# A graph network on one core: landing times in the planner, filled waits in front of bank sums, and a mask by TensorE

## The chip, the cores and the metric

The kernel runs on one core of a Trainium2 chip. A core has engines that run side by side, each with its own queue in order: TensorE (PE; its weight loads are shown as PEld), VectorE (DVE), ScalarE (ACT), GpSimd (POOL) and SyncE (SP), which here issues every DMA. They meet through semaphores. TensorE writes to PSUM banks; the other operands lie in SBUF. The metric is the device time of one execution in microseconds, as the median of several runs. The profile is one further execution with every instruction recorded.

## The reference

128 graphs of 128 nodes with 256 features each pass through two layers, all in f32.

```python
h = relu(layernorm(x))                       # layer 0: three steps of a gated network
for i in range(3):
    m = h @ weight[i]
    aggr = A^T @ m                           # A = (adj != 0), 128 x 128 per graph
    gi, gh = aggr @ w_ih.T + b_ih, h @ w_hh.T + b_hh
    r, z = sigmoid(i_r + h_r), sigmoid(i_z + h_z)
    n = tanh(i_n + r * h_n)
    h = (1 - z) * n + z * h
x = x + h
h = relu(layernorm(x))                       # layer 1: attention
Wh = h @ W.T
s1, s2 = Wh @ a1, Wh @ a2
e = leaky_relu(s1[:, None] + s2[None, :], 0.2); e = where(adj == 0, -inf, e)
x = x + softmax(e) @ Wh
```

The adjacency is symmetric and has its diagonal set.

## The kernel before

The graphs are worked on in 32 groups of four (`G = 4`, `NG = 32`; 512 columns, two halves of `H = 256`). A group g has a prologue (first norm, adjacency turned into 0 and 1, state transposed to columns), three steps `gru_step` (layers l = 0, 1, 2), and an epilogue (second norm and attention).

**A step.** The gates come from products of stationary 128x128 blocks with 256 moving columns (L705). Each 2x2 block product is done with seven products instead of four (as in Strassen's scheme), with sums in PSUM banks: `blocks` fills the banks `u` and `m7`, ScalarE copies `m7` out (L728), VectorE adds `c2 = u + m` (L731) and later `c22 = u + m` (L740). The bank `u` is written again by the next product, so each sum must have read it before. VectorE then adds halves of the candidate (`add_half`, L800), ScalarE applies tanh (L758, L793, L658), and VectorE makes the new state in three passes (L663, L665, L667). The sums' operands (`moving_sums`, L470) are VectorE's too. Steps of different groups are interleaved by a fixed plan (a step of layer l of group g stands at `3 g + 4 l`).

**Trips by way of DRAM.** A full transpose is made of 32x32 transposes on VectorE and a trip to DRAM and back (`by_way_of_dram`): four DMAs write z, four read it back. So go the state (`z_a`, `z`, `z_b`; writes of 128 KB) and the exponentials of the attention (`squares_by_blocks`, L586: `z_e<-prT`, then `e<-z_e`; writes of 64 KB). The gather on TensorE that reads e is `pq` (L614), and the last products `po` (L1063) follow. Groups 29, 30 and 31 (`late`) transpose on TensorE instead, without a trip; 30 and 31 (`end`) use tiles of other work, and 31 (`final_one`) goes in two halves of two graphs.

**The planner.** The order of instructions on all engines is written out at build time by `Order`, a list scheduler in Python with its own account of durations. Each piece of work is a generator that yields (engine, length, earliest start, tile to be free) ahead of each instruction; `begin` says when it could start, `take` books it, `issue` lets the generator go on. `HOP` is 0.2, `LAND` 2.5 us. `gru_step` drives it: after each product it fills with other tasks (`fill`, `matmuls`), by start and rank (`better`); the bank sums are booked with `take`, in the place of the program that they have. The account decides the order alone. At run time an instruction waits for what it needs, and whatever stands behind it in its queue waits too. What matters below: after its four writes `by_way_of_dram` sets the reads' earliest start to the last write plus `LAND`, and returns the last read plus `LAND`, whatever the size; `squares_by_blocks` adds 2.0 to that.

**Attention's mask.** `epilogue` makes scores with VectorE (L946), spreads them over the rows, adds the two and applies the leaky relu on ScalarE (L983); L992 turns A into 0 or -1e30, L994 adds it to e, L1000 takes the rows' maximum, L1004 the exponentials. In the last group relu is taken of x minus its mean alone (`norm_scales(..., True)`: L429, with the power on POOL, L431, beside it), and the scale rstd comes in later: in L946 and in the copies L1022.

Of the kernel before, what the change touches and what calls it, by code (L numbers as in the profile page):

```python
# [10 lines left out]
AF = mybir.ActivationFunctionType  # L11
ALU = mybir.AluOpType
# [5 lines left out]
G = 4  # L18
# [9 lines left out]
def preln_gnn_kernel(  # L28
# [144 lines left out]
    class Order:  # L173
# [18 lines left out]
        def take(self, engine, length, ready, room=None, count=1):  # L192
# [8 lines left out]
            return done  # L201

        def open(self, room, name):
            self.room_of[name] = room, self.next[room]
            self.next[room] = (self.next[room] + 1) % len(self.rooms[room])
            if room == "misc" and self.room_of[name][1] > 2:

                return more[self.room_of[name][1] - 3].rearrange("p n t -> p (n t)")
            if room == "misc":
                return ps_misc.tile([P, T], F32, tag="misc", name=name)  # L210
            if room == "h":
                return work.tile([P, G, D], F32, tag="h", name=name, bufs=ROWS)
# [66 lines left out]
        def finish(self, tasks=None, enough=lambda: False):  # L279

            tasks = self.tasks if tasks is None else [t for t in tasks if t[2] is not None]
            while tasks and not enough():
                best = None
                for task in self.tasks:
# [3 lines left out]
                    if engine == PE and start > self.free[PE] + 0.1 and task not in tasks:  # L288
                        continue
                    if self.better((start, rank), best):  # L290
# [121 lines left out]

    def norm_scales(src, graphs, ready, name, apart=False):

# [11 lines left out]
        put(nc.vector.tensor_scalar_add(rstd[:, all_], mv[:, all_, 1], EPS))  # L426
        if apart:
            t2 = yield DVE, 0.08, t - HOP
            put(nc.vector.tensor_scalar(nb[:, all_], mv[:, all_, 0], -1.0, None, ALU.mult))  # L429
            t = yield POOL, 1.05, t  # L430
            put(nc.gpsimd.tensor_tensor(rstd[:, all_], rstd[:, all_], mhalf[:, all_], ALU.pow))  # L431
            return rstd, nb, t2, t
        t = yield POOL, 1.05, t
# [7 lines left out]
    def norm_apply(src, graphs, rstd, nb, ready, name, kept, room="h"):  # L441

        for k in graphs:
            t = yield (ACT, 0.5, ready) if kept else (ACT, 0.5, ready, room)
            if not kept:
# [5 lines left out]
            put(nc.scalar.activation(  # L451
                h[:, k, :], src[:, k, :], AF.Relu, bias=nb[:, k : k + 1],
                scale=rstd[:, k : k + 1] if rstd is not None else 1.0,
            ))
# [60 lines left out]
    def by_way_of_dram(tmp, to, n, ready, name, room=None):  # L515

        z = None
        for i in range(Q):
# [3 lines left out]
            dma(z[:, :, i, :], tmp[i * 32 : (i + 1) * 32])  # L522
        order.close(f"tq_{name}" if n > G else f"prT_{name[:-2]}", t + LAND)
        ready = t + LAND
        rows_ = z.rearrange("r (q n) i a -> q r (n i a)", q=Q)
        to_ = None
        for q in range(Q):
# [3 lines left out]
            dma(to_[q * 32 : (q + 1) * 32], rows_[q])  # L531
        return t + LAND

# [48 lines left out]
    def squares_by_blocks(e, prT, ready, name):  # L582
# [5 lines left out]
        ))  # L588
        t = yield from by_way_of_dram(
            tmp.rearrange("p q k a -> p (q k) a"), lambda: e.rearrange("p k s -> p (k s)"),  # L590
            G, t, f"{name}_e",
        )
        return t + 2.0

# [59 lines left out]
    def state(s, o, old, new, v, z, ready):  # L654
# [5 lines left out]
        if len(s.halves) == C:  # L660
# [10 lines left out]
            if s.l < NL:  # L671
# [3 lines left out]
                if s.due:  # L675
                    s.task = order.add(0, inputs(s, s.hT_ready))
            else:

                for graphs in [range(G)] if s.g < NG - 1 else [range(2), range(2, 4)]:
                    order.add((1.8 if s.g >= NG - 2 else 1.9 if s.g == NG - 3 else 2), epilogue(s, graphs, max(s.halves)))  # L680

    def gru_step(s, last):
# [34 lines left out]
        def blocks(no, gates):  # L717
# [11 lines left out]
            done = product(gates, lambda q: u[:, q, :], S2, None, T2, t, False, (DVE,))  # L729
            t = order.take(DVE, 0.62, max(done, tm, banks["c2"]))  # L730
            put(nc.vector.tensor_tensor(c2, u, m, ALU.add))  # L731
# [6 lines left out]
            order.fill(t, (DVE,))  # L738
            tc22 = banks["u"] = order.take(DVE, 0.62, t)
            put(nc.vector.tensor_tensor(c22, u, m, ALU.add))  # L740
# [57 lines left out]
        def add_half(o, cols, src, ready):  # L798
            t = order.take(DVE, 0.38, max(ready, s.v_ready))
            put(nc.vector.tensor_tensor(v[:, o, cols], v[:, o, cols], src, ALU.add))  # L800
            return t
# [18 lines left out]
    class Group:  # L820


        def __init__(self, g):
            self.g, self.l, self.entered, self.aT = g, 0, False, None
            (self.xt, _), (self.at, self.at_ready) = xts.pop(g), ats.pop(g)
            self.scales = scales.pop(g)
            self.kept, self.prT = [], None
            self.e = self.hs = None
            self.due = False
# [29 lines left out]
    def prologue(s):  # L859
# [18 lines left out]
        if s.entered:  # L878
            s.task = order.add(0, inputs(s, s.hT_ready))

    def place_of_e(g):
        if g < NG - 2:
# [5 lines left out]
    def epilogue(s, graphs, ready):  # L888
# [21 lines left out]
        for i, two in enumerate(twos(graphs)):  # L910
# [7 lines left out]
            else:  # L918
                put(nc.vector.tensor_add(x1[:, k2, :], x1[:, k2, :], h[:, k2, :]))
        if final_one:  # L920

            rstd, nb, t, t2 = yield from norm_scales(x1, graphs, t - HOP, f"b{name}", True)
        else:
            rstd, nb, t = yield from norm_scales(x1, graphs, t - HOP, f"b{name}")
        h, t = yield from norm_apply(
            x1, graphs, None if final_one else rstd, nb, t, f"b{name}", s.kept,
            "tq" if end else "h",
        )
        if final_one:
            t = max(t, t2)  # L930

# [4 lines left out]
        for i in (1, 0):  # L936
            for k in graphs:
# [4 lines left out]
                if s.prT is None:  # L942
# [3 lines left out]
                put(nc.vector.scalar_tensor_tensor(  # L946
                    unused, h[:, k, :], rstd[:, k : k + 1] if final_one else 1.0, wa[:, i, :],
                    ALU.mult, ALU.mult,
                    accum_out=(one, two)[i][:, k : k + 1],
                ))  # L950

        if late:
            t = yield PE, graph_t, t, "misc"
            p2 = order.open("misc", f"ps2_{name}")
            for k in graphs:
                put(nc.tensor.transpose(
                    p2[:, k * P : (k + 1) * P], two[:, k : k + 1].to_broadcast([P, P]), ident
                ))
# [29 lines left out]
        le = e[:, part, :]  # L988

        off_ready = yield DVE, 0.36 * n / G, ready  # L990
        off = s.A[:, part, :]
        put(nc.vector.tensor_scalar(off, off, -1.0, BIG, ALU.add, ALU.mult))  # L992
        t = yield DVE2, row_t, max(t, off_ready) - HOP
        put(nc.vector.tensor_tensor(le, le, off, ALU.add))  # L994
        if s in live:
# [228 lines left out]
```

## Time and profile before

| | |
|---|---|
| Time, median of 3 runs | 2139.99 us (2139.34 to 2142.39) |
| The profiled execution: its own time | 2139.41 us |
| its span, first to last instruction | 2137.6 us |
| TensorE busy | 2117.2 us, 99% |
| VectorE busy | 1726.6 us, 81% |
| ScalarE busy | 1301.4 us, 61% |
| GpSimd busy | 103.5 us, 5% |
| DMA packets, bytes | 667973, 211.92 MB |
| mean granted clock of TensorE | 0.997 |

In the lines that follow, a row names an engine, a line of the kernel, the operation, the tile written and the tiles read, and their shapes; then how often, busy time and mean duration. A waiting row names who waited for whom, the total, how many times and the longest. In the order of time each row begins with its start and its length; brackets hold the engine's idle time before it and what ended it. SPq is SP's queue: the length there is the issue, not the transfer. Two matmul records belong to one f32 product, one to a transpose.

### The profile page before, as it was taken

The numbers are of one execution on the slowest core, as the hardware profiler recorded it, in microseconds if no ns is written. First come the engines' busy times: TensorE is split into PE (matmuls) and PEld (weight loads), VectorE is DVE, ScalarE is ACT, GpSimd is POOL, SyncE is SP. The second block draws the span as 40 slices with busy tenths as digits, with TensorE's granted clock in tenths as the row PEclk, the third lists the DMA queues.
The fourth block names the chain that finished last, engine by engine and source line by source line (L and its number), as shares of the span: only waits on it lengthen the run. The fifth ranks groups of instructions, "written<-read, shape, count | busy, mean of one in ns | idle before, by whom it ended". The sixth has DMA issues, their size and how long they took to land. (4 is left out here: it accounts for less than half of the span.)

```text
span 2137.6 us, 32105 instructions
## 1 busy us (share of the span) xinstructions
PE 2117.2 (99%) x10763; PEld 1878.8 (88%) x10763; DVE 1726.6 (81%) x3767; ACT 1301.4 (61%) x2855; POOL 103.5 (5%) x200
## 2 busy tenths in 40 slices
PE   9999999999999999999999999999999999999997
PEld 7888888888888888888888888888888888888886
DVE  7777888888878788878888787888778887787777
ACT  6556566565656566656656565666566565665664
POOL 1000000000000000000000000000000000000000
PEclk9999999999999999999999999999999999999998
DMA  5333453636353544545263536445462635344301
GB/s 158 64 85 83 88 117 70 154 65 141 90 121 73 133 96 94 125 111 119 56 149 82 120 72 137 88 98 122 95 133 64 146 82 107 84 88 108 84 19 46
DMA packets 667973, 211.92 MB, mean 99 GB/s; under 512 B 578336, under 2 KB 644640, under 8 KB 667808
## 3 DMA queue, kind: packets, MB, share of 16 engines
q1 hardware_dynamic: 667808, 209.87, 44.0%
q8 instruction: 85, 1.39, 0.3%
q14 instruction: 80, 0.66, 0.1%
HBM read 121.91 MB, written 87.88 MB: 98 GB/s over the span
## 5 line engine op out<-in xcount | busy, mean ns | idle before, releaser
L793 ACT ACTIVATE z<-c,brz 128x256 f32<-128x256 f32 x384 | 185.0, 482 | 305.4 <-PE c L705 158.5
L705 PE MATMUL u<-t_h,s_hh 128*128 128x256 f32 x1152 | 343.4, 380 | 0.3 <-DVE c L731 0.3
L705 PE MATMUL u<-t_a,s_f 128*128 128x256 f32 x1152 | 311.3, 379 | 0.0
L705 PE MATMUL c<-aT,s_f 128*128 128x256 f32 x1152 | 311.3, 379 | 0.0
L758 ACT ACTIVATE r<-c,brz 128x256 f32<-128x256 f32 x384 | 175.2, 477 | 207.7 <-PE c L705 127.3
L731 DVE TENSOR_TENSOR c<-u,m 128x512 f32<-128x512 f32 x192 | 134.0, 698 | 142.0 <-PE u L705 132.6
L705 PEld LDWEIGHTS u<-t_a,s_f 128*128 128x128 f32 x1152 | 218.9, 190 | 29.7
L705 PEld LDWEIGHTS c<-aT,s_f 128*128 128x128 f32 x1152 | 218.9, 190 | 29.7
L705 PEld LDWEIGHTS u<-t_h,s_hh 128*128 128x128 f32 x1152 | 216.7, 190 | 31.3 <-DVE c L731 2.2
L800 DVE TENSOR_TENSOR v<-v,c 128x256 f32<-128x256 f32 x384 | 154.4, 420 | 109.5 <-ACT z L793 55.3
L705 PE MATMUL c<-hT,s_hh 128*128 128x256 f32 x768 | 228.4, 379 | 0.0
L736 ACT COPY c<-u 128x512 f32<-128x512 f32 x192 | 109.4, 570 | 123.5 <-PE u L705 122.2
L728 ACT COPY m<-m 128x512 f32<-128x512 f32 x192 | 112.4, 585 | 105.1 <-PE m L705 105.1
L765 ACT ACTIVATE v<-c,bhn 128x256 f32<-128x256 f32 x384 | 172.1, 476 | 0.0
L705 PE MATMUL m<-t_h,s_hh 128*128 128x256 f32 x576 | 171.5, 379 | 0.0
L705 PE MATMUL c<-t_h,s_hh 128*128 128x256 f32 x576 | 171.3, 379 | 0.0
L740 DVE TENSOR_TENSOR c<-u,m 128x512 f32<-128x512 f32 x192 | 132.2, 688 | 42.3 <-ACT c L736 40.6
L705 PEld LDWEIGHTS c<-hT,s_hh 128*128 128x128 f32 x768 | 145.2, 190 | 19.4
L705 PE MATMUL m<-t_a,s_f 128*128 128x256 f32 x576 | 155.7, 379 | 0.0
L705 PE MATMUL u<-aT,s_f 128*128 128x256 f32 x576 | 155.7, 379 | 0.0
L705 PE MATMUL c<-t_a,s_f 128*128 128x256 f32 x576 | 155.6, 379 | 0.0
L652 DVE SCALAR_TENSOR_TENSOR v<-r,v 128x1024 f32<-128x1024 f32 x96 | 117.4, 1223 | 21.6 <-ACT v L765 20.0
(161 smaller groups left out, 3894.4 us busy)
## 6 DMA issues: line engine op xcount, KB each, us to landing
z<-tq SPq DMA_DIRECT2D x248, 128.0 KB
h<-z SPq DMA_DIRECT2D x248, 128.0 KB
xt<-in_x SPq DMA_DIRECT2D x31, 512.0 KB
z_a<-tq_a SPq DMA_DIRECT2D x120, 128.0 KB
hT_a<-z_a SPq DMA_DIRECT2D x120, 128.0 KB
z_b<-tq_b SPq DMA_DIRECT2D x116, 128.0 KB
h_b<-z_b SPq DMA_DIRECT2D x116, 128.0 KB
x<-in_x SPq DMA_DIRECT2D x29, 512.0 KB
```

Of the source, the lines that this page charges most:

```text
L652: put(nc.vector.scalar_tensor_tensor(flat(v), flat(r), 1.0, flat(v), ALU.add, ALU.mult))
L705: put(nc.tensor.matmul(to(q), S[0][:, gate_no, weight, :], moving, start=first and q == 0 and i == 0, stop=(i == len(ends) - 1), skip_grou ...
L728: put(nc.scalar.copy(m, m7))
L731: put(nc.vector.tensor_tensor(c2, u, m, ALU.add))
L736: put(nc.scalar.copy(c1[1], u))
L740: put(nc.vector.tensor_tensor(c22, u, m, ALU.add))
L758: put(nc.scalar.activation(r[:, o, cols], src, AF.Tanh, bias=brz[:, o : o + 1], scale=0.5))
L765: put(nc.scalar.activation(v[:, o, cols], src, AF.Identity, bias=bhn[:, o : o + 1], scale=0.5))
L793: put(nc.scalar.activation(z[:, o, cols], src, AF.Tanh, bias=brz[:, C + o : C + o + 1], scale=0.5))
L800: put(nc.vector.tensor_tensor(v[:, o, cols], v[:, o, cols], src, ALU.add))
```

## The change

**Landing by size.** `by_way_of_dram` sets the reads' earliest start to 3.7 us after the last write for trips of state (128 KB) and 1.8 us for e (64 KB), and returns 2.7 us after the last read; `squares_by_blocks` adds nothing to it any more.

**Filled waits.** A new `Order.fixed` books an operation whose place is given, but first issues other tasks of the same engine that end by the time at which it could begin, plus 0.1 us. The sums L731 and L740 and `add_half` use it. In `finish` a TensorE task that isn't ready is put last instead of being passed over.

**Mask by TensorE for groups 30 and 31.** A task `mask` makes A into 0 or -1e30 for the whole group, planned for 5 us before the last state half. `epilogue` puts a product of the identity with that A into the bank of the scores, and the scores are added to it by products instead of transposes; ScalarE reads the sum. For the other groups the mask stands as it did; group 29's scores are products too. VectorE's addition L994 falls away for 30 and 31.

**The last group's norm** is that of the others again: relu has the scale and the offset, L946 and the copy of the exponentials have none, and the copy is one for two graphs.

```diff
@@ class Order
+        def fixed(self, engine, length, ready):
+            while True:
+                until = ready + HOP
+                best = None
+                for task in self.tasks:
+                    if task[2][0][:3] != engine[:3]:
+                        continue
+                    start = self.begin(task[2][0], *task[2][2:])
+                    if start + task[2][1] <= until + 0.1 and self.better((start, task[0]), best):
+                        best = start, task[0], task
+                if best is None:
+                    return self.take(engine, length, ready)
+                self.issue(best[2])
@@ finish
                     if engine == PE and start > self.free[PE] + 0.1 and task not in tasks:
-                        continue
+                        start += 1000.0
@@ norm_scales
-        if apart:
-            t2 = yield DVE, 0.08, t - HOP
-            put(nc.vector.tensor_scalar(nb[:, all_], mv[:, all_, 0], -1.0, None, ALU.mult))
-            t = yield POOL, 1.05, t
-            put(nc.gpsimd.tensor_tensor(rstd[:, all_], rstd[:, all_], mhalf[:, all_], ALU.pow))
-            return rstd, nb, t2, t
@@ by_way_of_dram
-        order.close(f"tq_{name}" if n > G else f"prT_{name[:-2]}", t + LAND)
-        ready = t + LAND
+        ready = t + (3.7 if n > G else 1.8)
+        order.close(f"tq_{name}" if n > G else f"prT_{name[:-2]}", ready)
...
-        return t + LAND
+        return t + 2.7
@@ squares_by_blocks
-        t = yield from by_way_of_dram(
+        return (yield from by_way_of_dram(
...
-        return t + 2.0
@@ state
+                if s.g >= NG - 2:
+                    s.off_ready = INF
+                    order.add(1, mask(s, max(s.halves) - 5.0))
@@ blocks (the same for c22), add_half
-            t = order.take(DVE, 0.62, max(done, tm, banks["c2"]))
+            t = order.fixed(DVE, 0.62, max(done, tm, banks["c2"]))
...
-            t = order.take(DVE, 0.38, max(ready, s.v_ready))
+            t = order.fixed(DVE, 0.38, max(ready, s.v_ready))
@@ new
+    def mask(s, ready):
+        t = s.off_ready = yield DVE, 0.36, ready
+        put(nc.vector.tensor_scalar(s.A, s.A, -1.0, BIG, ALU.add, ALU.mult))
+        return t
@@ epilogue
-        if final_one:
-            rstd, nb, t, t2 = yield from norm_scales(x1, graphs, t - HOP, f"b{name}", True)
-        else:
-            rstd, nb, t = yield from norm_scales(x1, graphs, t - HOP, f"b{name}")
+        rstd, nb, t = yield from norm_scales(x1, graphs, t - HOP, f"b{name}")
...
-                    unused, h[:, k, :], rstd[:, k : k + 1] if final_one else 1.0, wa[:, i, :],
-                    ALU.mult, ALU.mult,
+                    unused, h[:, k, :], 1.0, wa[:, i, :], ALU.mult, ALU.mult,
...
         if late:
-            t = yield PE, graph_t, t, "misc"
+            t = yield PE, 4 * graph_t if end else graph_t, max(t, s.off_ready), "misc"
             p2 = order.open("misc", f"ps2_{name}")
+            if end:
+                put(nc.tensor.matmul(
+                    p2[:, cols], ident, s.A[:, part, :].rearrange("p k s -> p (k s)"),
+                    start=True, stop=False, skip_group_check=True,
+                ))
             for k in graphs:
-                put(nc.tensor.transpose(
-                    p2[:, k * P : (k + 1) * P], two[:, k : k + 1].to_broadcast([P, P]), ident
+                put(nc.tensor.matmul(
+                    p2[:, k * P : (k + 1) * P], two[:, k : k + 1].to_broadcast([P, P]), ident,
+                    start=not end, stop=True, skip_group_check=True,
                 ))
...
-        off_ready = yield DVE, 0.36 * n / G, ready
-        off = s.A[:, part, :]
-        put(nc.vector.tensor_scalar(off, off, -1.0, BIG, ALU.add, ALU.mult))
-        t = yield DVE2, row_t, max(t, off_ready) - HOP
-        put(nc.vector.tensor_tensor(le, le, off, ALU.add))
+        if not end:
+            off_ready = yield from mask(s, ready)
+            t = yield DVE2, row_t, max(t, off_ready) - HOP
+            put(nc.vector.tensor_tensor(le, le, s.A, ALU.add))
...
+            t = yield ACT, bank_t, t
+            order.close(f"pp_{name}", t)
             prT = s.prT
-            if not final_one:
-                t = yield ACT, bank_t, t
-                put(nc.scalar.copy(prT[:, part, :].rearrange("p k s -> p (k s)"), pp[:, cols]))
-            else:
-                ready = t
-                for k in graphs:
-                    t = yield ACT, 0.3, ready
-                    put(nc.scalar.activation(
-                        prT[:, k, :], pp[:, k * P : (k + 1) * P], AF.Identity,
-                        scale=rstd[:, k : k + 1],
-                    ))
-            order.close(f"pp_{name}", t)
+            put(nc.scalar.copy(prT[:, part, :].rearrange("p k s -> p (k s)"), pp[:, cols]))
```

More of the change, by code (lines that the diff above doesn't have):

```diff
@@ L410, in preln_gnn_kernel, with norm_scales @@
     s_hh, s_f = (stationary_tile("hh"), {}), [(stationary_tile(f"f{l}"), {}) for l in range(NL)]
-    def norm_scales(src, graphs, ready, name, apart=False):
+    def norm_scales(src, graphs, ready, name):
         st = small.tile([P, G, 6], F32, tag="st", name=f"st_{name}", bufs=2)
@@ L451, in norm_apply @@
             put(nc.scalar.activation(
-                h[:, k, :], src[:, k, :], AF.Relu, bias=nb[:, k : k + 1],
-                scale=rstd[:, k : k + 1] if rstd is not None else 1.0,
+                h[:, k, :], src[:, k, :], AF.Relu, bias=nb[:, k : k + 1], scale=rstd[:, k : k + 1]
             ))
@@ L588, in squares_by_blocks @@
         ))
-        t = yield from by_way_of_dram(
+        return (yield from by_way_of_dram(
             tmp.rearrange("p q k a -> p (q k) a"), lambda: e.rearrange("p k s -> p (k s)"),
             G, t, f"{name}_e",
-        )
-        return t + 2.0
+        ))
     def rows(s, ready, name):
@@ L738, in blocks @@
             order.fill(t, (DVE,))
-            tc22 = banks["u"] = order.take(DVE, 0.62, t)
+            tc22 = banks["u"] = order.fixed(DVE, 0.62, t)
             put(nc.vector.tensor_tensor(c22, u, m, ALU.add))
@@ L826, in __init__ @@
             self.scales = scales.pop(g)
+            self.off_ready = 0.0
             self.kept, self.prT = [], None
@@ L919, in epilogue @@
                 put(nc.vector.tensor_add(x1[:, k2, :], x1[:, k2, :], h[:, k2, :]))
-        if final_one:
-            rstd, nb, t, t2 = yield from norm_scales(x1, graphs, t - HOP, f"b{name}", True)
-        else:
-            rstd, nb, t = yield from norm_scales(x1, graphs, t - HOP, f"b{name}")
+        rstd, nb, t = yield from norm_scales(x1, graphs, t - HOP, f"b{name}")
         h, t = yield from norm_apply(
-            x1, graphs, None if final_one else rstd, nb, t, f"b{name}", s.kept,
-            "tq" if end else "h",
-        )
-        if final_one:
-            t = max(t, t2)
+            x1, graphs, rstd, nb, t, f"b{name}", s.kept, "tq" if end else "h"
+        )
         v = small.tile([P, 2, G], F32, tag="s", name=f"s_{name}")
@@ L952, in epilogue @@
         if late:
-            t = yield PE, graph_t, t, "misc"
+            t = yield PE, 4 * graph_t if end else graph_t, max(t, s.off_ready), "misc"
             p2 = order.open("misc", f"ps2_{name}")
+            if end:
+                put(nc.tensor.matmul(
+                    p2[:, cols], ident, s.A[:, part, :].rearrange("p k s -> p (k s)"),
+                    start=True, stop=False, skip_group_check=True,
+                ))
             for k in graphs:
-                put(nc.tensor.transpose(
-                    p2[:, k * P : (k + 1) * P], two[:, k : k + 1].to_broadcast([P, P]), ident
+                put(nc.tensor.matmul(
+                    p2[:, k * P : (k + 1) * P], two[:, k : k + 1].to_broadcast([P, P]), ident,
+                    start=not end, stop=True, skip_group_check=True,
                 ))
```

## The prediction

> **What bounds the kernel now.** I read the page first, for the engine that is full; then TensorE's waits, for the places where it isn't; then the order of time around the largest kind of wait; then windows of the last 30 us.
>
> ```profile
> span 2137.6 us, 32105 instructions
> PE 2117.2 (99%) x10763; PEld 1878.8 (88%) x10763; DVE 1726.6 (81%) x3767; ACT 1301.4 (61%) x2855; POOL 103.5 (5%) x200
> ```
>
> TensorE is busy for 99% of the span. A busy PE need not be at its peak, so I checked the work behind it. Six passes of a 128x256 product stand in 1.29 us in the chain, 0.2157 us each; an f32 product has two passes, 0.431 us, a 128x128 one 0.222 us, a transpose one pass of 0.111 us. A group of four graphs has 3 x 42 products for the steps (18.1 us each step, 54.4), 24 for the sums over neighbours (5.3), 8 for the attention (1.8) and 8 for the output (3.5): 64.9 us, and 32 groups fill the span. So only TensorE's waits and what stands at both ends can be won. VectorE's idle time is mostly in front of the bank sums (132.6 us until L705), but L731 held TensorE up once, for 0.3 us.
>
> ```profile
> engine line waited for: us in total, times, longest us
> PE pq L614 <- DMA e<-z_e: 5.9, 6, 1.7
> PE c L956 <- DVE prT L946: 4.4, 1, 4.4
> PE u L504 <- DVE hT L667: 3.7, 1, 3.7
> PE pw L362 <- DMA wih<-in_w_ih_t: 1.4, 2, 1.2
> ```
>
> The first row is in the middle of the kernel, the next two are the end. The order of time around the longest of the six, and around a trip of another group that waits for nothing:
>
> ```profile
> 1288.07 0.70 DVE L586 STREAM_TRANSPOSE prT<-e 128x512 f32<-128x512 f32 x1
> 1288.51 2.50 SPq L60 DMA_DIRECT2D hT_a<-z_a  x4
> ...
> 1292.15 2.49 SPq L60 DMA_DIRECT2D h<-z  x4
> 1294.74 3.52 SPq L60 DMA_DIRECT2D z_e<-prT  x4
> ...
> 1300.07 1.70 SPq L60 DMA_DIRECT2D e<-z_e  x4
> ...
> 1303.93 0.35 PE L614 MATMUL pq<-e,h_b 128*128 128x128 f32 x1 [1.74 <-DMA e<-z_e]
> ...
> 1172.26 0.70 DVE L586 STREAM_TRANSPOSE prT<-e 128x512 f32<-128x512 f32 x1
> 1172.99 2.92 SPq L60 DMA_DIRECT2D z_e<-prT  x4
> 1176.64 2.87 SPq L60 DMA_DIRECT2D z<-tq  x4
> 1179.69 2.40 SPq L60 DMA_DIRECT2D e<-z_e  x4
> ```
>
> In the first, the transpose is done at 1288.8 but SP still has another group's writes and reads in hand, and the writes of e go out 6.7 us after the transpose's start instead of 0.7. The six trips that wait are those where SP was 6 to 7 us late (groups 7, 10, 13, 16, 19, 22). In the second, SP is free; e's last read is issued 9.8 us after the transpose, and TensorE takes e 14.4 us after it without a wait.
>
> ```profile
> 2105.00:2111.00 6.00, 2.40 (x12) 1.76 (x10) 5.63 (x13) 1.27 (x3) 0.00 (x0) 1.00 0.00 0
> 2111.00:2113.00 2.00, 1.56 (x12) 1.29 (x12) 1.95 (x6) 0.26 (x1) 0.00 (x0) 0.88 0.00 0
> 2113.00:2117.00 4.00, 0.00 (x0) 0.00 (x0) 3.81 (x12) 2.04 (x7) 0.89 (x1) 0.50 0.00 0
> 2119.00:2122.40 3.40, 3.40 (x10) 2.64 (x9) 2.52 (x11) 2.30 (x7) 0.84 (x1) 0.50 0.16 57
> ```
>
> These are windows (us, then PE, PEld, DVE, ACT, POOL, then the granted clock). The last product of the last step ends at 2105.5; VectorE is then full while TensorE idles twice, the granted clock falls to 0.50, and eight passes of po take 3.41 us in the chain instead of 1.73. From 2105.5 to the span's end are 32.1 us, for 16.6 us of TensorE's work.
>
> **The change, part by part.**
>
> *Accounts of writes.* Nothing in an instruction changes; the planner's order does, and each trip's 8 DMAs go with it. In the new order of instructions I counted TensorE's products between the one that VectorE's transpose stands behind and the first product that reads e. Before, it is 14.2 to 16 us by group, with z_e behind other groups' trips in every third. After, groups 1 to 26 all have 16.0 us and one SP order: z_e, z of another state (128 KB), e, h. That is the second excerpt, which nine trips already have, none with a wait. Its margin: reads issued by +10.0 us at worst, landing 1.7 to 2.8 us after the last issue (the six late trips), product at +14.4: 1.6 us to spare. The queue that z_e was moved past is SP's, which is free then: its preceding load comes some 20 us earlier. So the six waits go. Their worth: 5.9 us of rows, but from group 5's transpose to group 23's (584.00 to 1761.58) are 1177.6 us for 18 x 64.93 = 1168.7 us of products, a difference of 8.9, of which 1.2 may be the rounding of the pass (0.1%): 7.7 lost. Between 5.9 and 7.7 I take 7.2, as each wait seems to cost 0.2 more than its row. What is late next: the trips of h have 26 us or more of products in front of them (21 before). Group 27 is bunched: z_e between two writes of z_b, and only 12.2 us to its product against some 10 to 11 us of trip: 0 to 1.2 us, I take 0.4.
>
> *Filling in front of bank sums.* It moves work within VectorE; the same instructions remain. TensorE pays only if a sum comes late: it is read 0.32 us after the sum's end in nearly every case. The fill lets work end 0.1 us after the sum could begin; walking VectorE's order with the rows' durations, one sum per group (behind four L470 at 0.45 us) lands where eight of before landed, which TensorE awaited by 0.05 us at most. So 0 to 1.2 us in all, I take 0.1, and 0.2 for the first 60 us, where VectorE's order is a little longer.
>
> *Mask by TensorE.* Removed behind L946: L992, L994 (0.42 and 0.69 for four graphs, 0.28 and 0.43 for two), now one row of 0.42 per group, made earlier (for group 31 right behind hT, ahead of the maximum of 30's e). Added: the mask's products, 0.86, 0.43 and 0.43 us, and twelve transposes of scores turned into two-pass products, 12 x 0.11: 3.1 us of TensorE's work. No row of before has this mask product; the nearest is L705's width, 0.216 us a pass of 256, and twice that for 512. The product waits for A alone; behind it on TensorE stand the scores, then attention of group 29.
>
> *Scale taken back into the last group's norm.* The relu waits for POOL's three operations, some 0.7 to 0.9 + 0.27 + 0.2 us, instead of none: about 1.2 us later. The two scaled copies L1022 (0.63) become one of 0.37. Cover of the 1.2: TensorE's po of groups 29 and 30, 3.4 us, which the new order puts before the last scores. Without that cover, +1.2.
>
> *The end, summed.* Before the last product of a step, TensorE has 2088.4 us of products where it had 2089.7: 1.3 earlier. Then, from that product's end: mask and scores of 30, attention of 29 to 3.5 us; idle to 6.0 (v, z and two tanh to 2.4, then three passes of hT at 1.14 and the hop; before, 5.6); transposes and po of 29 to 8.6; e of 30 to 9.1; a copy, idle to 10.0; attention of 30, po of 29 and 30 to 15.2 without a gap; scores of 31 to 16.1, po of 30 to 17.8, scores of its second half and e to 18.9; then three short waits for copies (0.7 each) and 5.5 us of products to 26.4. With the 3.4 us that stand between TensorE's last product and the end of the span now, 29.8 us, against 32.1: 2.3 won.
>
> *The clock, row against rule.* In before the clock fell after 3.74 us idle plus 1.6 us of transposes. The Trainium skill (TensorE: Matmul & The Clock Gate, What's actually happening) says that half clock comes after at least one idle window of about 3.4 us, and (Part 4: PE-mode transpose) that transposes do not count as busy like products. After the change the stretch is 2.45 us idle and 0.9 us of transposes, 3.3. By the row (5.3 us fell) nothing is said of 3.3; by the rule it stands just under the bound, and the window runs free, so it mostly holds. Full clock gives the 29.8 above; half clock adds 1.7, the row's 3.41 less 1.73. I take full clock.
>
> Sum: 2137.6 - 7.2 - 1.3 - 2.3 + 0.4 + 0.1 + 0.2 = 2127.5 us of span. The profiled execution took 2139.4, 1.8 more than its span, and the median of the runs is 0.6 over it: 2129.9.
>
> **Rivals.**
>
> *The end gives nothing* (20%). The clock falls, or VectorE's longer queue (hT behind three scores and an output row) moves the idle times rather than shortening them: then 2.3 to 4 us come back, 2132 to 2134. For it: a stretch of 3.3 us so near the window; VectorE 5.63 of 6 us busy. Against: more of TensorE's work stands ready for the hole, 3.5 us for 1.7.
>
> *Waits of e return in part* (7%): SP's trips land more slowly where they now follow each other, half of the 7.2 stays and group 27 costs 1.2: 2134 to 2137. Against: the nine trips.
>
> *A wait in each group, slower* (5%). The account for e's writes allows 1.8 + 2.7 us where it allowed 7. If e now lands later than 14.4 us after its transpose in every period, 27 trips make TensorE wait. Each wait costs its length and 0.2; it decides at 10.1 / 27 = 0.37 us a group, a landing at 14.6 us; with waits of 0.7 us it is 2129.9 + 27 x 0.9 = 2154. Against: 1.6 us to spare in the nine.
>
> *It does nothing* (3%): the planner's order is fixed by TensorE, fills are off its path: 2139 to 2141. The fills alone are this; the change of SP's order is not.
>
> **How the numbers follow.** The likeliest, all of the sum, has 65%, with 2126 to 2132 of its own (at the one end 7.7 won by the waits and 5.0 at the end, if half of the 5.4 us of idle time that my walk leaves there goes too; at the other 5.9 and 1.5, with all extras). About 0.2%, 4.3 us, is what a measurement can tell from no change: faster means under 2135.7. That holds for the likeliest, the first rival and half of the second: 0.89. Within: the rest of the second and the third's nothing, 0.06. Slower 0.05. The range, 2125.5 to 2135, has 0.5 below that for the median's own spread and leaves out the last two rivals and half of the second.
>
> **What would show it.** TensorE's row for e<-z_e at 0 to 1 us, and only group 27 in it. Every z_e issued 0.7 us after its transpose. The row c L731 under 1.5 us. At the end one idle stretch near 2.5 us in place of 3.7 and 4.4, granted clock 1.00 in it, and the span's end 29 to 31 us after the last product of a step. The forecast is wrong if the row of e grows to a wait per group, if bank sums hold TensorE for several us, or if the clock halves.

## The result, and the profile after

The changed kernel takes 2128.83 us (median of six, 2128.43 to 2129.86) beside 2140.05 us (2138.60 to 2144.93) for the kernel before: 0.9944 of it, with an interval of 0.9931 to 0.9957. The forecast was 2129.9. The total was right. The reason given for its largest part was not, and one term at the end was a matter of chance.

The head of the page of the changed kernel; its profiled execution took 2129.86 us, 1.8 more than its span:

```profile
span 2128.1 us, 32183 instructions
PE 2117.1 (99%) x10781; PEld 1885.4 (89%) x10781; DVE 1723.9 (81%) x3761; ACT 1300.5 (61%) x2853; POOL 101.9 (5%) x204
```

TensorE's waits after the change (who waited for whom, us in total, times, longest):

```profile
PE u L513 <- DVE hT L676: 2.5, 1, 2.5
PE pw L378 <- DMA wih<-in_w_ih_t: 1.5, 2, 1.3
PE c L623 <- ACT prT L1033: 1.2, 2, 0.7
PE c L146 <- DVE zero L139: 1.2, 1, 1.2
PE u L717 <- DVE c L743: 0.5, 1, 0.5
PE u L717 <- ACT c L737: 0.4, 2, 0.2
```

The row of 5.9 us for e<-z_e is gone, group 27 included. The row of 4.4 us for the last scores is gone too, and the wait for hT (the last group's state, which TensorE turns back into rows) is 2.5 us instead of 3.7. The order of time around the trip of group 16, which had the longest wait before (VectorE's transpose, SP's queue, TensorE):

```profile
1278.52 0.70 DVE L596 STREAM_TRANSPOSE prT<-e 128x512 f32<-128x512 f32 x1
...
1279.26 2.57 SPq L60 DMA_DIRECT2D z_e<-prT  x4
1282.91 2.96 SPq L60 DMA_DIRECT2D z<-tq  x4
1286.04 2.37 SPq L60 DMA_DIRECT2D e<-z_e  x4
1288.59 1.69 SPq L60 DMA_DIRECT2D h<-z  x4
...
1292.94 1.95 PE L623 MATMUL pq<-e,h_b 128*128 128x128 f32 x16
```

SP has nothing else in hand: z_e goes out 0.74 us after the transpose's start where it was 6.7, the last read of e is issued 9.9 us after that start (+9.9 from here on), and the product stands at +14.42. All of groups 1 to 26 have this shape, with the last read between +9.8 and +11.0.

Windows of the end of the changed kernel (us, then PE, PEld, DVE, ACT, POOL, then the granted clock), and TensorE's order of time there:

```profile
2096.00:2101.00 5.00, 4.18 (x29) 3.43 (x28) 4.31 (x12) 4.09 (x10) 0.00 (x0) 1.00 0.24 86
2101.00:2104.00 3.00, 1.28 (x10) 1.26 (x11) 2.97 (x5) 0.37 (x2) 0.00 (x0) 1.00 0.09 32
2104.00:2107.00 3.00, 3.00 (x10) 2.24 (x9) 2.66 (x10) 1.28 (x8) 1.10 (x3) 0.50 0.00 0
2107.00:2110.00 3.00, 2.33 (x18) 2.03 (x17) 2.63 (x13) 2.04 (x4) 1.21 (x4) 0.93 0.00 0
```

```profile
2096.48 1.02 PE L968 MATMUL ps<-A,ident 128*128 128x512 f32 x2
...
2102.72 0.66 PE L513 MATMUL u<-ident,hT 128*128 128x128 f32 x4 [2.54 <-DVE hT L676]
2103.21 0.60 PE L513 MATMUL m<-ident,hT 128*128 128x128 f32 x4
2103.65 3.27 PE L1070 MATMUL c<-gwt,hs 128*128 128x256 f32 x8
```

The last product of a step ends at 2096.5 instead of 2105.5. There is one idle stretch, of 2.54 us, but behind it the clock falls to 0.50 and the eight passes of po take 3.27 us. From the last product of a step to the end of the span are 31.6 us; 32.1 before, 29.8 forecast.

For the comparisons below one number is worked out for each kernel: how much later than at full clock, without any wait, TensorE stands at a place. It is the product's start in the trace less the time of all products before it (0.2157 us for a pass of 256 columns). I read what is lost between 60 and 2085 us of products (the body; what comes before 60 differs by up to 2.3 us between executions of one kernel), and from there to TensorE's end.

| kernel | TensorE's products | lost in the body | lost at the end |
|---|---|---|---|
| before | 2106.1 | 10.3 | 12.3 |
| accounts alone | 2106.1 | 75.6 | 12.2 |
| fills alone | 2106.1 | 3.2 | 13.7 |
| mask and norm alone | 2109.2 | 10.9 | 11.9 |
| accounts and fills | 2106.1 | 3.4 | 15.4 |
| fills, mask and norm | 2109.2 | 3.1 | 9.1 |
| accounts, mask and norm | 2109.2 | 75.7 | 12.5 |
| the whole change (three profiles) | 2109.2 | 3.2, 3.2, 3.2 | 7.5, 7.2, 7.5 |

### The profile page after: what moved, and what is told of

Its sections match the earlier page's. It is cut to its first block, busy times and chain, and to the rows that moved or that the text cites. A ratio compares the mean times of both kernels' runs of the same rounds, so it can differ in the third digit from the quotient of the medians.

```text
span 2128.1 us, 32183 instructions
## 1 busy us (share of the span) xinstructions
PE 2117.1 (99%) x10781; PEld 1885.4 (89%) x10781; DVE 1723.9 (81%) x3761; ACT 1300.5 (61%) x2853; POOL 101.9 (5%) x204
## 4 chain that ended last, share of the span: by engine, by line
PE 98%; DVE 1%; ACT 1%; DMA 0%; issue 0%; POOL 0%; SPq 0%; ACTq 0%
PE c L717 35%; PE u L717 35%; PE m L717 12%; PE pa L623 8%; PE po L1070 5%; PE pq L623 2%; PE pw L378 0%; PE c L1070 0%; DMA xt<-in_x 0%; ACT v L667 0%; DVE st_a L436 0%; PE pr_o L513 0%; PE pr L513 0%; PE m L1070 0%; PE pw_a L418 0%; DVE t_h L479 0%
## 5 line engine op out<-in xcount | busy, mean ns | idle before, releaser
L743 DVE TENSOR_TENSOR c<-u,m 128x512 f32<-128x512 f32 x192 | 134.3, 700 | 129.2 <-PE u L717 128.9
L740 ACT COPY m<-m 128x512 f32<-128x512 f32 x192 | 112.4, 585 | 116.0 <-PE m L717 116.0
L748 ACT COPY c<-u 128x512 f32<-128x512 f32 x192 | 109.4, 570 | 96.2 <-PE u L717 95.9
L737 ACT COPY c<-u 128x512 f32<-128x512 f32 x192 | 109.5, 570 | 70.4 <-PE u L717 70.3
```

The costliest lines, as they stand in the source:

```text
L737: put(nc.scalar.copy(c1[0], u))
L740: put(nc.scalar.copy(m, m7))
L748: put(nc.scalar.copy(c1[1], u))
```

## The experiments

**Accounts alone.** The kernel before with the new times in `by_way_of_dram` and `squares_by_blocks`, and the line in `finish`.

```diff
+        ready = t + (3.7 if n > G else 1.8)
...
-        return t + LAND
+        return t + 2.7
...
-        return t + 2.0
+        return t
```

> The kernel before with the landing accounts alone (3.7 and 1.8 us after the writes, 2.7 after the reads), and a TensorE task that is not ready put last in finish. Theory of the prediction, that the accounts give the one order of SP and so take the six waits away: TensorE's waits for e near 0, 2132 us (8 less than before). Rival, that the fills in front of VectorE's booked sums make the order regular: in this kernel's order of instructions e's trips have between 11.6 and 16.0 us of products, and every seventh group has twelve other DMAs between the transpose and its own; it should wait there 3 to 5 us, at 3 or 4 groups, and lose the other six waits: 2138 to 2150 us, no faster than before.

Measured: 2203.95 us (2203.22 to 2205.76), 1.0306 of before (1.0290 to 1.0321). The accounts alone lose 65 us, which neither the theory nor the rival had. TensorE's waits of this kernel:

```profile
PE u L707 <- ACT c L727: 64.8, 5, 21.7
PE u L505 <- DVE hT L669: 4.0, 1, 4.0
```

There is no row for e<-z_e, so the six waits are gone here as well. In their place a bank copy of a step (L727, `c1 = u` on ScalarE) holds TensorE up three times, for 21.3 to 21.7 us, ending at 769, 1248 and 1727 us. The order of time of the first, from SP's, ScalarE's and TensorE's rows:

```profile
753.97 2.16 SPq L60 DMA_DIRECT2D line<-score  x4
...
759.28 0.73 SPq L60 DMA_DIRECT2D e<-line  x1
763.24 1.28 ACT L985 ACTIVATE e<-e,s 128x128 f32<-128x128 f32 x4 [17.50 <-DMA e<-line]
...
768.55 0.58 ACT L727 COPY c<-u 128x512 f32<-128x512 f32 x1
769.19 1.22 PE L707 MATMUL u<-t_h,s_hh 128*128 128x256 f32 x2 [21.31 <-ACT c L727]
```

ScalarE's queue has the leaky relu of an attention (L985), its exponentials and the copies of hs ahead of the bank copy. The relu waits 17.5 us for the scores' line from DRAM, which SP can't write to DRAM and fetch any earlier because VectorE has the scores only at 751.8. The product whose sum it copies had ended at 746.6. Two passes then take 1.22 us instead of 0.59, and in all the first stall costs 23.9 us of TensorE's time. Why the planner wrote that order is the question of the experiment with seven tiles below.

**Fills alone.** The kernel before with `fixed` for the two sums and `add_half`.

```diff
-            t = order.take(DVE, 0.62, max(done, tm, banks["c2"]))
+            t = order.fixed(DVE, 0.62, max(done, tm, banks["c2"]))
```

> The kernel before with the fills in front of VectorE's sums alone, the accounts as they were (2.5 us after the writes, 4.5 after the reads of e). Theory of the prediction: fills are off TensorE's path, 2139 to 2141 us with the six waits for e. Rival: the fills make every group's order alike (16.0 us of products in each trip of groups 1 to 26, SP free at the transpose): no wait for e, z_e issued 0.7 us after the transpose, 2131 to 2133 us.

Measured: 2133.62 us (2132.72 to 2136.39), 0.9976 of before (0.9966 to 0.9986). TensorE's longest waits of this kernel:

```profile
PE c L971 <- DVE prT L961: 6.9, 2, 6.7
PE pw L377 <- DMA wih<-in_w_ih_t: 1.5, 2, 1.2
PE po L1078 <- ACT hs L1070: 1.4, 1, 1.4
```

No e<-z_e either, though the accounts are the old ones: z_e goes out 0.73 us after its transpose in groups 1 to 26, as in the whole change. The body loses 3.2 us instead of 10.3. Part of that is given back at the end (13.7 for 12.3), where the last scores come 6.7 us late instead of 4.4. The regular order of SP that the forecast put down to the accounts is thus the fills' doing.

**The whole change without the fills.** The same at the three places.

```diff
-            t = order.fixed(DVE, 0.62, max(done, tm, banks["c2"]))
+            t = order.take(DVE, 0.62, max(done, tm, banks["c2"]))
```

> The whole change with the fills in front of bank sums undone (the sums are booked as before). The accounts alone lost 65 us by three stalls of TensorE of some 21 us; in the planner's own account this kernel has those three stalls at the same places, TensorE's 747, 1227 and 1708 us. Theory: the fills are what keeps the accounts from this, so the run takes about 2139.5 + 63, between 2199 and 2205, with a bank copy of the gates on ScalarE as the reason of three waits of 21 us. Rival: with the mask by TensorE and its other order at the end, or by chance of the planner, the stalls go, and the run takes 2129 to 2140.

Measured: 2207.46 us (2207.23 to 2209.55), 1.0320 of before (1.0306 to 1.0334). Again a bank copy of a step is the longest row of TensorE's waits, and the clock averages 0.982:

```profile
PE u L717 <- ACT c L737: 65.3, 5, 21.7
```

The mask by TensorE does not lift the stalls, and with accounts and mask in it, it is the fills that keep them out.

**Seven tiles of h.** When the planner's account is printed as it writes the accounts-only kernel, it shows three places in the middle, at 747.1, 1227.4 and 1707.7 us of its TensorE time. There `settle` (it prepares the step that comes next) needs a state's rows, and the read of the trip (h<-z) can't be booked. Three of the six tiles of h are free, but they are taken in a fixed turn, and the tile whose turn it is belongs to an attention that isn't issued yet (of group 7, 14 and 21). So `finish` books that attention as far as its product, ScalarE's part too, and only then begins the step. Fills alone and the whole change show no such place between 90 and 2037 us. A seventh tile shifts the turn. To test it I gave the accounts-only kernel one, with room from m and c22, which have one buffer instead of two; the planner's account knows nothing of m and c22, so the new order comes from the seventh tile alone:

```diff
-    ROWS = 6
+    ROWS = 7
...
-            m = gate.tile([P, 2, H], F32, tag="m", name=f"m_{name}_{no}")
-            c22 = gate.tile([P, 2, H], F32, tag="c22", name=f"c22_{name}_{no}")
+            m = gate.tile([P, 2, H], F32, tag="m", name=f"m_{name}_{no}", bufs=1)
+            c22 = gate.tile([P, 2, H], F32, tag="c22", name=f"c22_{name}_{no}", bufs=1)
```

> The accounts alone (with the line in finish), which lost 65 us, but with seven tiles for h instead of six; the room for it comes from m and c22, which have one tile instead of two. Theory: at three places the planner needs a tile of h for a state's trip while the sixth is held by an attention that has not been issued, and then writes that attention's ScalarE work ahead of the next bank copy. With seven tiles its own account has no such place in the middle of the kernel, so the three waits of 21 us for a bank copy vanish and the run takes 2132 to 2145 us, whatever a single m and c22 cost within that. Rival: the stalls come from the accounts' times themselves and not from the tiles; then it takes 2190 or more.

Measured: 2137.16 us (2135.22 to 2138.80), 0.9985 of before (0.9975 to 0.9995); the line in `finish` is left out in it, which makes no difference to its order of instructions. TensorE's longest waits of this kernel:

```profile
PE pr_o L504 <- DVE hT L668: 5.6, 1, 5.6
PE pw L362 <- DMA wih<-in_w_ih_t: 1.8, 2, 1.4
PE c L615 <- ACT prT L1018: 1.3, 1, 1.3
```

The planner's account shows none of the three places any more, the stalls of 21 us are gone, and the waits for e as well: the body loses 3.4 us. So it was the turn of the tiles, and not the times in themselves. Accounts and fills each take the six waits away; the accounts do it only where the tile in turn is free, and not by the one order that was forecast: here z_e goes out 0.73 to 3.24 us after its transpose in groups 1 to 26, and the product stands between +10.0 and +13.6. The end is poor here (17.8 us lost), with 5.6 us for hT.

**Mask and norm alone.** The kernel before with the mask by TensorE, the plain norm of the last group, and the line in `finish`.

```diff
+                put(nc.tensor.matmul(
+                    p2[:, cols], ident, s.A[:, part, :].rearrange("p k s -> p (k s)"),
+                    start=True, stop=False, skip_group_check=True,
+                ))
```

> The kernel before with the mask by TensorE and the last group's norm alone; accounts and fills as before, so the middle's order is that of before. Both theories: the six waits for e stay. If the end wins by its shorter VectorE chain: 2137 to 2139 us. If the end's gain in the changed kernel comes from the order that the fills give it: 2140 us, within 1 us of before.

Measured: 2142.15 us (2139.72 to 2144.92), 1.0013 of before (1.0003 to 1.0023). The waits for e stand at 6.4 us in six, as they must. TensorE has 3.1 us more work and loses only 0.4 us less at the end: on its own this part costs something, where 2137 to 2140 were expected.

**The whole change without the accounts.** The old times at the three places; the fills, the line in `finish`, mask and norm stay.

```diff
-        ready = t + (3.7 if n > G else 1.8)
-        order.close(f"tq_{name}" if n > G else f"prT_{name[:-2]}", ready)
+        order.close(f"tq_{name}" if n > G else f"prT_{name[:-2]}", t + LAND)
+        ready = t + LAND
...
-        return t + 2.7
+        return t + LAND
```

> The changed kernel with the old accounts back (2.5 us after the writes, 4.5 after e's reads), fills and mask kept. Theory of the prediction: the order of SP falls back, six waits for e, 2136 to 2138 us. Rival (fills): the order of the middle stays regular, no wait for e, 2128 to 2131 us; only the end may differ, since 3.5 us more of TensorE's work stand in front of the last product of a step.

Measured: 2131.15 us (2130.96 to 2132.56), 0.9965 of before (0.9952 to 0.9978). With the fills in place the mask and the norm are worth 2.5 us (2133.62 to 2131.15 on one chip): the end loses 9.1 us instead of 13.7, for 3.1 us of work. hT then holds TensorE up for 2.0 us, the scores no longer.

**Accounts and fills, with the old end.** The kernel before with the edits of the first two experiments together, so against the whole change:

```diff
-            if end:
-                put(nc.tensor.matmul(
-                    p2[:, cols], ident, s.A[:, part, :].rearrange("p k s -> p (k s)"),
-                    start=True, stop=False, skip_group_check=True,
-                ))
...
+        off_ready = yield DVE, 0.36 * n / G, ready
+        off = s.A[:, part, :]
+        put(nc.vector.tensor_scalar(off, off, -1.0, BIG, ALU.add, ALU.mult))
```

> The accounts, the fills and the line in the planner's finish, with the old mask and the old norm of the last group. The sum of parts: the fills alone gave 2133.62, and the accounts took 2.3 us from the kernel that has fills and mask (2131.15 to 2128.83). If that gain is the accounts' own, this run takes 2131.3 and ends 1.4 us or so later than the whole change. Rival one: the gain needs the mask by TensorE, and this run stays at 2133.6. Rival two: mask and norm are worth nothing at all and this run equals the whole change, 2128.8.

Measured: 2135.01 us (2134.94 to 2135.48), 0.9968 of before (0.9956 to 0.9981), beside 2130.13 for the whole change on the same chip. The first rival holds, since all kernels are slower on this chip: the kernel before takes 2141.17 us here, so the gain is 6.2, beside 5.7 for the fills alone, where before took 2139.30. The accounts' gain in company of the mask (2131.15 to 2128.83, on two chips; 1.6 to 1.9 us at the end in the traces) needs the mask. Without it the end loses 15.4 us, with one idle stretch of 4.6 for hT and half clock after it. Here the mask and the norm are worth 4.9 us. The parts do not add up: what each is worth at the end depends on how the planner packs the others there.

**The norm of the last group put back.** The whole change with the old `norm_scales(..., True)`, the scale in the scores and in two copies.

```diff
+            rstd, nb, t, t2 = yield from norm_scales(x1, graphs, t - HOP, f"b{name}", True)
...
-                    unused, h[:, k, :], 1.0, wa[:, i, :], ALU.mult, ALU.mult,
+                    unused, h[:, k, :], rstd[:, k : k + 1] if final_one else 1.0, wa[:, i, :],
+                    ALU.mult, ALU.mult,
```

> The whole change, with the old norm of the last group (relu of x minus the mean, scale in the scores and in two copies) put back. Theory: the 1.2 us that the norm costs is hidden behind the po of groups 29 and 30 on TensorE, which reaches the last scores about 3 us after VectorE has them; so the span stays within 0.3 us of the whole change, 2128.8, or is up to 0.3 later for the second copy. Rival: the norm was on the path and this run is 1.2 us shorter, 2127.6.

Measured: 2129.75 us (2128.97 to 2130.90), 0.9943 (0.9931 to 0.9956), beside 2130.13 (2129.15 to 2131.63). There is no gain of 1.2 us that could be told from nothing. Its profile is the one, of those with this idle stretch, in which the clock held:

```profile
2104.05 0.66 PE L520 MATMUL u<-ident,hT 128*128 128x128 f32 x4 [2.54 <-DVE hT L683]
2104.54 0.60 PE L520 MATMUL m<-ident,hT 128*128 128x128 f32 x4
2104.98 1.89 PE L1093 MATMUL c<-gwt,hs 128*128 128x256 f32 x8
```

The same 2.54 us, the same transposes, and po takes 1.89 us. From the last product of a step to the end are 30.4 us. So the length of the stretch alone doesn't settle whether the clock falls.

**Products in the idle stretch.** The whole change with five products of 128x256 (their result is overwritten) ahead of the transposes that wait for hT; the whole change itself ran beside it. Both were done twice, on two chips.

```diff
+            if name == "31_0_o" and two[0] == 0:
+                for _ in range(5):
+                    put(nc.tensor.matmul(pt[:, 0, :], ident, gwt[:, 0, :], start=True, stop=True))
```

> The whole change, with five products of 128x256 (2.16 us by 0.431 each) put into TensorE's idle stretch of 2.54 us near the end; their result is overwritten. Theory: the idle stretch is what lets the clock fall. Then the clock stays at 1.00 through it, the eight passes of po of group 29 take 1.75 to 1.9 us instead of 3.27, and the span ends 1.3 us earlier, about 2127.5 where the whole change takes 2128.8. Rival: the clock falls whatever TensorE does there, or the products delay the transposes behind them: 2128.8 to 2129.5, with the po still at 3.2 or later.

> The whole change, unaltered, beside the other three on the same chip: 2128.8, span 2128, with TensorE's wait of 2.5 us for hT and the po of group 29 at 3.27 us in its trace.

> The five products in the idle stretch once more, beside the whole change on the same chip. Theory: the clock stays at 1.00 to the end again, from the last product of a step to the end of the span are 29.9 us, and the median is 0.8 to 1.5 us under that of the whole change. Rival: the first comparison was chance, and the two are within 0.3 us.

> The whole change, unaltered, a third time. Theory: TensorE idles for 2.54 us each time, and whether the clock falls behind it depends on where the stretch lies; with a fall the end takes 31.4 to 31.6 us from the last product of a step, without it 29.9. The median lies 0.8 to 1.5 us over that of the run with products in the stretch, if the clock falls in most executions; with the clock held in all of them there is no difference.

Measured: 2128.78 us (2128.04 to 2129.32) beside 2130.13 (2129.15 to 2131.63) on the first chip, 2129.19 (2128.40 to 2130.03) beside 2129.30 (2128.63 to 2129.62) on the second. Against before: 0.9938 (0.9926 to 0.9951) and 0.9943 (0.9930 to 0.9957), then 0.9952 (0.9940 to 0.9965) and 0.9951 (0.9938 to 0.9965). Windows with the products in the stretch, first chip:

```profile
2101.00:2104.00 3.00, 2.62 (x14) 2.01 (x14) 2.97 (x4) 0.70 (x2) 0.00 (x0) 1.00 0.36 126
2104.00:2107.00 3.00, 2.79 (x18) 2.30 (x16) 2.79 (x8) 1.82 (x9) 0.37 (x1) 1.00 0.00 0
2107.00:2110.00 3.00, 2.53 (x19) 2.46 (x20) 2.68 (x13) 2.42 (x5) 1.83 (x6) 1.00 0.03 5
```

and its order of time on TensorE:

```profile
2100.83 2.32 PE L513 MATMUL u<-gwt,ident 128*128 128x256 f32 x10
2103.54 0.66 PE L516 MATMUL u<-ident,hT 128*128 128x128 f32 x4 [0.38 <-DVE hT L679]
2104.03 0.60 PE L516 MATMUL m<-ident,hT 128*128 128x128 f32 x4
2104.47 1.89 PE L1073 MATMUL c<-gwt,hs 128*128 128x256 f32 x8
```

The clock stays at 1.00, po takes 1.89 us, and from the last product of a step to the end are 29.9 us, in both profiles. With work in the stretch the clock doesn't fall, so the cause is shown; its worth is smaller than expected, and the second comparison is the rival's. Each execution's mean clock tells why. The whole change ran sixteen times in all: in nine the mean is 1.000 and the times are 2128.43 to 2129.30 (median 2128.86), in seven it is 0.999 and they are 2129.51 to 2131.63 (median 2129.86). With the products it is 1.000 in all ten. Between the medians a fall costs 1.0 us. It comes in seven of sixteen, in one of six of the first set and in four and two of five of the others; all three profiled executions are among the seven. The products spare the fall, and I see nothing else that they bring: their medians, 2128.78 and 2129.19, stand beside the 2128.86 of the nine. So this version isn't measurably faster than the whole change in every set.

## Why the prediction was right or wrong

**The six waits, -7.2: right in size.** The body loses 3.2 us instead of 10.3, 7.1 won. The extra of 0.2 on each row holds: rows of 5.9 cost 7.1. The margin held as well, though the last reads came up to 1.0 us later than the +10.0 that I had as the worst, and group 27 waits for nothing in the whole change, though its product stands at +10.6, earlier than the 12.2 that I counted. In three profiles of sibling kernels with the same accounts (the norm put back, and both with products in the stretch) it lost 0.2 to 0.4 us, so the 0.4 was a fair bound.

**Who takes them away: wrong.** The step that failed is "Nothing in an instruction changes; the planner's order does, and each trip's 8 DMAs go with it", under the heading of the accounts, with its counterpart "The fills alone are this; the change of SP's order is not". I compared the order of the whole change with the order of before and gave the difference on SP to the edit that speaks of SP. The fills alone make that order, at 0.9976 of before; that rival ("It does nothing") was thus stated on a false ground. The accounts alone also remove the waits, and lose 65 us by something that is in no step of mine: in the planner's account a tile is still held when its turn comes, and the order that it then writes has three stalls behind a bank copy. No rival named it. The 7.2 survived because it was counted on the order of the whole change, in which both edits stand; for the accounts by themselves, the reason given for it would have missed by 72 us. The rival of a slower end was a landing of e, which never came near.

**The fills' own price, 0.1 and 0.2: slightly low.** VectorE's late sum costs 0.5 us in one row (c L743), in the first 60 us, and two late bank copies on ScalarE 0.4 (c L737). Near 2030 us of products one of these, a row of 0.2, costs 0.5; kernels without the accounts lack it.

**The end, -1.3 and -2.3: right at full clock.** Measured in the same account, the end of before loses 12.3 us and that of the whole change 7.5, for 3.1 more of products: 1.7 won instead of 3.6. With the clock held by products in the stretch it loses 5.8: 3.4 won, and 29.9 us from the last product of a step where I had 29.8. The mis-sized term is the clock, and the 1.7 that I had named for it is its size in the profiles. Why the medians with and without a fall lie only 1.0 apart is not shown.

**The clock, row against rule: right in nine executions of sixteen.** I took full clock, as the stretch of 3.3 us stood just under the bound of the Trainium skill (TensorE: Matmul & The Clock Gate, What's actually happening) of about 3.4. The stretch measured 2.54 us idle and 0.93 of transposes, 3.47. But a window of 3.4 us that runs free would lie wholly inside 3.47 us only rarely (an estimate from the two lengths), not in seven of sixteen. The traces show that so long a stretch isn't needed. In the second profile of the whole change the granted clock is 0.50 from 2104.29 on, 2.07 us after the end of TensorE's last product (pq), and the transposes behind the idle stretch already run at half clock, 1.12 and 1.06 us instead of 0.66 and 0.60:

```profile
2100.26 1.95 PE L623 MATMUL pq<-prT,h_b 128*128 128x128 f32 x16
2104.76 1.12 PE L513 MATMUL u<-ident,hT 128*128 128x128 f32 x4 [2.54 <-DVE hT L676]
2105.66 1.06 PE L513 MATMUL m<-ident,hT 128*128 128x128 f32 x4
2106.52 2.48 PE L1070 MATMUL c<-gwt,hs 128*128 128x256 f32 x8
```

So po took 2.48 us there and not the 3.27 that I expected of it. In the first profile the fall comes at 2104.01, 3.83 us after the last product and with 0.36 us of po done. In the first stall of the accounts alone it comes 2.05 us after the last product, at 749.92. That the window runs free agrees with the traces: within a profile the recorded changes of the clock lie whole multiples of 3.413 us apart (2104.01 and 2107.42 in the first profile; 2112.52 and 2122.76, three times as far, in the kernel before). So I was wrong to hold the summed length against a bound. Where a stretch lies in this grid decides as well, and that differs from one execution to the next (2.07 and 3.83 us from the last product to the fall). How much work in a window keeps the clock up isn't shown.

**The norm's 1.2 us: right.** The po of groups 29 and 30 cover it: VectorE is done with the first of group 31's scores at 2110.7, and TensorE reaches their bank, with the mask, at 2113.7.

**The sum.** 2127.5 us of span were forecast. The five executions of the first set with a held clock have spans of 2126.6 to 2127.4. The 0.6 that I added for the median over the profile was before's own: after the change the profiled execution had the fall and lies above the median, not under it. And the working added up parts that don't add: alone they give +65, -5.7 and +2.9 us, together -11.2.

## What to carry to other kernels

A list scheduler's times are part of the kernel: an account that is nearer the truth can still meet a tile that is held when its turn comes, and put an engine's waiting work ahead of an urgent copy. When a change has several edits that act through one planner, build each edit alone and compare the orders before giving a gain to the one whose name fits it. Look in the planner for places where it is forced to book work out of turn, and in the trace for long waits on an engine that is only half busy.

## What was not expected of the hardware

An engine that is busy for 59% of the span (ScalarE, accounts alone) held TensorE up for 21 us, because one instruction at the head of its queue waited 17.5 us for a DMA. A short wait of TensorE costs more than its row: six rows, 5.9 us in all, cost 7.1, and one of 0.2 cost 0.5. And the same transposes and po behind the same idle stretch of 2.54 us ran at half clock in one profile (po 3.27 us) and at full clock in another (1.89 us). An idle stretch of 2.07 us was enough for a fall.
